# Decay tables woven into the first projection, and q of the first direction loaded in alternating pieces

## The chip, the cores and the metric

The program runs on one core of a Trainium2 chip. The metric is the time of one execution on the device in microseconds (us). Work is done by TensorE (PE; its weight loads are listed as PEld), VectorE (DVE), ScalarE (ACT) and GpSimd (POOL). Transfers between the chip's main memory and the on-chip memory of 128 rows (partitions) are issued by SyncE (SP) and by POOL, each in its own order, and run on 16 DMA engines which all queues share.

## The reference

The input x has 8 samples of 56 x 56 positions with 192 channels. Four layers follow each other, each of the form x = x + layer(group norm of x). Layers 0 and 1 are the ones concerned here. Each computes, with D = 576 channels:

```
p, q, v = silu(x @ p_w.T + p_b), silu(x @ q_w.T + q_b), silu(x @ v_w.T + v_b)
a1 = mlp1(lags) * decay ;  a2 = mlp2(lags) * decay      # (111 lags, D): one value per lag and channel
o1 = toeplitz(q * v, a1) along the width ;  o2 = toeplitz(q * v, a2) along the height
out = (p * (o1 + o2)) @ o_w.T + o_b
```

toeplitz(y, a) is, per channel, y multiplied by the 56 x 56 matrix that has a(i - j) at row i and column j. The decay of a lag n is a power n of a number per channel. Layer 2 is a depthwise 7 x 7 convolution with a two-layer product, layer 3 a window attention. Everything is float32.

## The kernel before, in words

The two Toeplitz layers are cut into generators which a hand-written weaver interleaves. `tno_qv` (called Q) projects two pairs of samples to q and v and stores q*v in main memory (`qv`); its products are at L260, or at L281 for the first 512 positions, where the two pairs are done one after the other (`apart`). `tno_toeplitz` (TZ) multiplies by the Toeplitz matrices, and `tno_out` (O) makes p, the gate and the output product. Per layer there are two halves of the batch (`j0` 0 and 2). The stages are: Q(0,0) alone; TZ(0,0) woven with Q(0,2); TZ(0,2) woven with O(0,0) and Q(1,0); TZ(1,0) woven with O(0,2) and Q(1,2); TZ(1,2) woven with O(1,0); and the last O woven with the convolution of layer 2.

**The start.** `input_stats` loads x of each of four pairs in seven tiles (L119, seven buffers) and DVE takes their statistics (L215). Q(0,0) starts when pair 0 has its norm. `decay_tables` (L134 on) makes the tables of one layer: powers of the decay on DVE, then for each of two directions three small products through the mlp (L179) and five products for the channels (L185), each followed by DVE's writes of the tile `a` (L192, two buffers) and by two to four stores of `a` into the table in main memory (L202, 36 stores per layer, 120 KB each). Each table step is built without a pause in the program: first all of layer 0 after 24 steps of Q, then 14 steps of Q with the statistics of pairs 2 and 3, then all of layer 1. A zero tile is made ahead of layer 1's tables and POOL copies it (L715) into the rows of `qv` behind the 56 x 56 positions, since loads of the second direction fetch 64 rows, and (L719) into the end of each table. In this part a scheduler orders each engine's instructions by their dependencies and by their place in the program; in the Toeplitz stages the compute engines follow the order of the program.

**Toeplitz.** A stage has 18 steps: nine blocks of 64 channels, two directions each. A step needs a q tile of 128 rows (q*v of two times 64 channels and samples: rows 0 to 55 and 64 to 119 are used; two buffers) and a matrix tile `tm` (two, used in turn). For the first direction rows of q are positions along the width: two transfers (L376), each of 56 rows with 56 runs of 512 bytes. For the second direction one transfer (L379) of 128 rows of 28,672 bytes. `tm` comes in four transfers of 32 rows of 7,680 bytes, for every fourth row each (L389). All are issued by SP, and a step's loads are issued when the last product of the step two before has been issued. SP waits for what an instruction needs before it goes on to the next, and the built order shows that each of its transfers also waits for the one eight before it. Products are at L402, ACT takes them out of PSUM (L409), DVE transposes them (L420, L422), and POOL adds the second direction (L424) and stores the sum.

The lines of q's load before the change:

```
for half in range(2):
    of = qv[2 * blk + half, :T].rearrange("(h w) e -> w h e", w=W)
    nc.sync.dma_start(q[64 * half : 64 * half + W], of)
```

Of the kernel before, what the change touches and what calls it, by code (L numbers as in the profile page):

```python
# [38 lines left out]
def view(ap, offset, dims):  # L39

    return bass.AP(ap.tensor, ap.offset + offset, [ap.ap[0], *dims])


class Net:
# [91 lines left out]
    def decay_tables(self, L, p, tables):  # L136
# [5 lines left out]
        for c in range(5):  # L142
            m = min(128, D1 - 128 * c)
            sl = p.tile([128, 1], F32, name="sl")
            nc.sync.dma_start(sl[:m], inp[f"{L}_slope"][128 * c : 128 * c + m, :])
            nc.vector.tensor_scalar(sl[:m], sl[:m], 0.0, 1.0, ALU.max, ALU.min)
            nc.vector.tensor_scalar(sl[:m], sl[:m], 1.0 - 0.95, 0.95, ALU.mult, ALU.add)
            pw = p.tile([128, 64], F32, name="pw", bufs=5)
            nc.gpsimd.memset(pw[:m, 0:1], 1.0)
            n = 1  # L150
            while n < 64:
                nc.vector.tensor_scalar(
                    pw[:m, n : 2 * n], pw[:m, 0:n], sl[:m], None, ALU.mult
                )
                n *= 2
                if n < 64:
                    sq = p.tile([128, 1], F32, name="sl")
                    nc.vector.tensor_mul(sq[:m], sl[:m], sl[:m])
                    sl = sq
            pows.append(pw)  # L160
        for d in range(2):
            t = f"{L}_t{d + 1}"
            w0 = p.tile([32, 2], F32, name="w0")
# [13 lines left out]
            for i in range(3):  # L177
                hp = self.bank2()[:32, 0, :111]
                nc.tensor.matmul(hp, ws[:, i, :], h, start=True, stop=True)  # L179
                h = p.tile([32, 111], F32, name="h")  # L180
                nc.vector.tensor_scalar(h, hp, bs[:, i : i + 1], 0.0, ALU.add, ALU.max)
            for c in range(5):
                m = min(128, D1 - 128 * c)
                ap = self.bank2()[:, 0, :111]
# [15 lines left out]
                for n in range(m // 32):  # L200
                    to = tables[d][self.TG * (4 * c + n) : self.TG * (4 * c + n + 1)]
                    nc.sync.dma_start(  # L202
                        to.rearrange("g (c w) -> c g w", w=self.TW),
                        view(a[32 * n : 32 * n + 32], 0, [[4, self.TG], [1, self.TW]]),
                    )

    def input_stats(self, xs, gn, j, p):

# [153 lines left out]
    def tno_toeplitz(self, j0, mats, qv, o):  # L362
# [6 lines left out]
        def load(n):  # L369
            blk, d = divmod(n, 2)  # L370
            q = p.tile([128, H, 128], F32, name="q", bufs=2)
            if d == 0:

                for half in range(2):
                    of = qv[2 * blk + half, :T].rearrange("(h w) e -> w h e", w=W)
                    nc.sync.dma_start(q[64 * half : 64 * half + W], of)  # L376
            else:
                of = qv[2 * blk : 2 * blk + 2].rearrange("n (h w) e -> (n h) (w e)", w=W)
                nc.sync.dma_start(q.rearrange("p i e -> p (i e)"), of)  # L379
            return q  # L380

        def matrices(n):

            blk, d = divmod(n, 2)
            row = 32 * self.TW
            at = mats[d].offset + 2 * blk * self.TG * row
            for k in range(4):
                of = bass.AP(mats[d].tensor, at + k, [[row, 2 * self.TG], [1, row]])
                nc.sync.dma_start(self.tms[n % 2][k:128:4], of)  # L389

        def along(n, q, ot, g):

# [44 lines left out]
        loaded = []  # L437
        for n in range(2):
            loaded.append(load(n))
            matrices(n)  # L440
        yield 8.0

        work = []
# [10 lines left out]
        for n in range(NS):  # L454
# [4 lines left out]
            for g in range(8):  # L459
# [5 lines left out]
                if g % 2:  # L465
                    if g == 7 and n + 2 < NS:
                        loaded.append(load(n + 2))
                        matrices(n + 2)
                    yield 3.2
                    behind()  # L470
        while work:
# [194 lines left out]
    def tno_layers(self, x0, x1, x2, gn, last):  # L666
# [18 lines left out]
        with ExitStack() as ctx, ExitStack() as wqp:  # L685
# [7 lines left out]
            with tc.tile_pool(name="tab", bufs=2) as tab:  # L693
# [10 lines left out]
                    pass  # L704
                for n in range(10):
                    next(first)
                self.decay_tables("L0", tab, tables[0])
                for st in stats[2:]:
                    for more in st:
                        next(first)  # L710
                none = tab.tile([112, 512], F32, name="none", bufs=1)
                nc.gpsimd.memset(none, 0.0)
                for qv in qvs.values():
                    to = qv[:, T:].rearrange("n (p k) e -> p n (k e)", p=112)
                    nc.gpsimd.dma_start(to, view(none, 0, [[0, D1 // 32], [1, 512]]))  # L715
                self.decay_tables("L1", tab, tables[1])
                for t in tables:
                    for d in range(2):
                        nc.gpsimd.dma_start(t[d][D1 // 32 * self.TG :, :512], none[:1])  # L719
                lanes = [[(first, QT - 104.0)], [(Q(0, 2), QT)], [(O(0, 0), OT), (Q(1, 0), QT)]]  # L720
                lanes += [[(O(0, 2), OT), (Q(1, 2), QT)], [(O(1, 0), OT)], [(O(1, 2, False), OT)]]
                self.weave(lanes[0], None, lanes[1][0][0])
            in_order = tc.manual_schedule(engines=ENGINES)
            with tc.tile_pool(name="tz", bufs=1) as self.tz, in_order:
                self.tms = []
# [915 lines left out]
```

## Time and profile before

| what | us |
|---|---|
| median of 3 runs (5851.6 to 5859.38) | 5857.68 |
| the profiled execution | 5859.99 |
| its span, first to last instruction | 5858.2 |
| PE busy in the span | 5356.5 (91%) |
| first product of Q(0,0) | 52.68 |
| first Toeplitz product (L402) | 507.7 |

The profile is of one execution. A line of the windows view gives the stretch, its length, and for PE, PEld, DVE, ACT and POOL the busy time with the number of instructions in brackets, then the mean granted clock of PE (1.00 is full), the mean busy share of the 16 DMA engines (packets overlap, so it can exceed 1) and GB/s. A line of the timeline gives start, length, engine, line of the code and operation; in square brackets the idle time before it and what ended it. SPq lines are the issue of transfers by SP, and their length is how long SP was held, not how long the data took. The trace also holds one record for each DMA packet, with its start, duration, size and queue.

### The profile page before, as it was taken

To read this page: it belongs to the slowest core of one execution; us is meant where nothing else is said; L and a number is where in the kernel's file an instruction comes from. 1 tells how busy PE (TensorE), PEld (TensorE's weight loads), DVE (VectorE), ACT (ScalarE), POOL (GpSimd) and SP (SyncE) were. 2 spreads that over 40 slices of the span, in tenths; PEclk is the share of its full clock that TensorE was granted. 3 is DMA by queue.
4 is the path that set the end of the run, shared out by engine and by line. 5 is a ranking of instruction groups with operands and counts; after the bars stand their busy time and mean duration, and the time that the engine had idled before them with its cause. 6 is when DMAs were issued, how large, how long until landed. Compare 5 with 4: busy or idle time off the path is not lost.

```text
span 5858.2 us, 144266 instructions
## 1 busy us (share of the span) xinstructions
PE 5356.5 (91%) x64672; PEld 3886.7 (66%) x64672; DVE 2365.6 (40%) x3770; ACT 2269.0 (39%) x2990; POOL 2206.4 (38%) x1527
## 2 busy tenths in 40 slices
PE   5799888899999999999888799989999999889887
PEld 2577666677777777777666578856665445667666
DVE  5444554233454233553343322331222322556655
ACT  2244454444454444554444322242323333333332
POOL 1244566466556564565666300000001001333332
PEclk8799999999999999999999899999999999999998
DMA  8547998898787887987999465644444222344442
GB/s 268 110 144 219 267 287 245 220 264 275 214 237 217 239 258 224 254 249 196 312 296 293 168 210 205 230 125 161 150 160 121 64 64 62 75 97 86 89 92 56
DMA packets 1029770, 1098.79 MB, mean 188 GB/s; under 512 B 232768, under 2 KB 966976, under 8 KB 1013728
## 3 DMA queue, kind: packets, MB, share of 16 engines
q1 hardware_dynamic: 993568, 888.57, 55.5%
q0 software_dynamic: 35584, 200.99, 8.9%
q8 instruction: 509, 8.34, 0.6%
q14 instruction: 109, 0.89, 0.0%
HBM read 725.48 MB, written 363.94 MB: 186 GB/s over the span
## 4 chain that ended last, share of the span: by engine, by line
PE 57%; POOL 6%; SPq 6%; DMA 5%; DVE 5%; issue 3%; ACT 2%; POOLq 0%; DVEq 0%; ACTq 0%
PE bank L260 9%; PE bank L950 6%; PE bank L811 5%; PE bank L527 4%; PE bank L1030 4%; PE bank L572 4%; PE bank L402 4%; SPq L389 3%; PE bank L1044 3%; POOL s L424 2%; PE bank L1224 2%; PE bank L536 2%; PE bank L575 2%; SPq L376 2%; PE bank L1171 2%
## 5 line engine op out<-in xcount | busy, mean ns | idle before, releaser
L260 PE MATMUL bank<-wq,t 128*128 128x256 f32 (+4 forms) x7680 | 1286.6, 375 | 66.8 <-DVE t L269 36.3
L260 PEld LDWEIGHTS bank<-wq,t 128*128 128x128 f32 (+2 forms) x7680 | 1006.5, 191 | 348.1 <-issue 110.5
L269 DVE TENSOR_TENSOR t<-bank,wq 128x1024 f32<-128x1024 f32 (+3 forms) x480 | 517.8, 1111 | 776.6 <-PE bank L260 575.1
L301 POOL TENSOR_TENSOR t<-t 128x1024 f32<-128x1024 f32 (+2 forms) x288 | 518.7, 1815 | 692.4 <-ACT t L298 371.5
L409 ACT COPY ot<-bank 128x896 f32<-128x896 f32 x576 | 493.2, 914 | 626.8 <-PE bank L402 351.3
L424 POOL TENSOR_TENSOR s<-s,ot 128x1568 f32<-128x1568 f32 x144 | 618.3, 4298 | 70.0 <-DVE ot L422 69.3
L402 PE MATMUL bank<-q,tm 56*32 56x224 f32 x18432 | 525.6, 365 | 81.6 <-DMA tm<-L_tab 26.8
L298 ACT ACTIVATE t<-t 128x2048 f32<-128x2048 f32 (+2 forms) x288 | 422.0, 1488 | 405.7 <-DVE t L269 396.1
L402 PEld LDWEIGHTS bank<-q,tm 56*32 56x32 f32 x18432 | 354.4, 109 | 221.6 <-issue 115.8
L553 POOL TENSOR_TENSOR t<-t,t 128x896 f32<-128x896 f32 x168 | 347.3, 2085 | 358.4 <-DMA t<-L_sum 163.9
L527 PE MATMUL bank<-t,wo 128*128 128x224 f32 x1792 | 398.0, 378 | 46.6 <-ACT t L506 22.1
L585 DVE SCALAR_TENSOR_TENSOR t<-bank,wo,t 128x448 f32<-128x448 f32 x112 | 76.4, 682 | 886.3 <-ACT t L581 474.7
L950 PE MATMUL bank<-z,w 128*128 128x448 f32 (+1 forms) x1344 | 413.7, 555 | 1.9 <-ACT h L959 1.7
L527 PEld LDWEIGHTS bank<-t,wo 128*128 128x128 f32 x1792 | 352.4, 203 | 83.8 <-issue 31.7
L546 ACT ACTIVATE t<-bank,wo 128x448 f32<-128x448 f32 x448 | 248.1, 635 | 407.2 <-PE bank L536 379.2
L572 PE MATMUL bank<-t,wo 128*128 128x224 f32 x1792 | 378.1, 365 | 0.0
L127 POOL DMA_DIRECT2D x<-x x64 | 36.6, 573 | 859.7 <-DVE x L981 829.6
L572 PEld LDWEIGHTS bank<-t,wo 128*128 128x128 f32 x1792 | 337.2, 194 | 33.8 <-issue 32.2
L811 PEld LDWEIGHTS bank<-xt,cm 113*112 113x112 f32 x3072 | 315.0, 180 | 43.7 <-issue 38.3
L420 DVE STREAM_TRANSPOSE s<-ot 128x1792 f32<-128x1792 f32 x144 | 292.5, 2033 | 124.3 <-DMA L_sum<-s 102.1
L811 PE MATMUL bank<-xt,cm 113*112 113x108 f32 (+2 forms) x3072 | 326.2, 266 | 6.4 <-issue 3.3
L950 PEld LDWEIGHTS bank<-z,w 128*128 128x128 f32 (+1 forms) x1344 | 182.2, 189 | 205.7 <-issue 197.4
(148 smaller groups left out, 6991.3 us busy)
## 6 DMA issues: line engine op xcount, KB each, us to landing
q<-qv SPq DMA_DIRECT2D x36, 3584.0 KB
q<-qv SPq DMA_DIRECT2D x72, 1568.0 KB
L_sum<-s POOLq DMA_DIRECT2D x288, 392.0 KB, 7.4
t<-L_sum SPq DMA_DIRECT2D x112, 1008.0 KB
qv<-t SPq DMA_DIRECT2D x192, 512.0 KB
cm<-in_L_cm SPq DMA_DIRECT2D x96, 896.0 KB
tm<-L_tab SPq DMA_DIRECT2D x288, 240.0 KB
x<-t POOLq DMA_DIRECT2D x112, 336.0 KB, 7.1
```

The source lines that it names most:

```text
L260: nc.tensor.matmul(pp[:m, b, 256 * j : 256 * j + k], x[rows, j, 2 if part else b, s : s + m], w[rows, part, c0 + c : c0 + c + k],  start=p ...
L269: nc.vector.tensor_add(z[:m, c : c + k, :], view(pp[:m], 0, [[1, k], [256, 4]]), view(bias[:m], c0 + c, [[1, k], [0, 4]]),)
L298: nc.scalar.activation(z[:m, :n, :], z[:m, :n, :], AF.Silu)
L301: nc.gpsimd.tensor_mul(prod[:m, :k], half[:, :, 0], half[:, :, 1])
L402: nc.tensor.matmul(pt[32 * j : 32 * j + 32, r, hf * 224 : (hf + 1) * 224], tm[rows, at : at + 32], q[rows, :, 4 * c : 4 * c + 4], start=Tr ...
L409: nc.scalar.copy(view(ot, 4 * (g % 4), [[16, 2], [32, 112], [1, 4]]), view(pt, 0, [[512, 2], [4, 112], [1, 4]]),)
L424: nc.gpsimd.tensor_add(to, to, view(of, 0, [[1, 28], [32, 56]]))
L527: mm(gs[c // 2][:, b, c % 2 * 256 : c % 2 * 256 + N], pw[:, 0, 128 * c : 128 * c + 128], xn[:, b], start=c % 2 == 0, stop=False,)
L553: gate.tensor_mul(to, to, pg)
L572: mm(P[:, b, :N], ow[:, c, 0:128], g[:, 4 * b + c], start=False, stop=c == 3 and b == 1)
L811: nc.tensor.matmul(pc[:, 128 * e + 4 * m0 : 128 * e + 4 * m1], cm[:113, e, k, :], xt[:, m0 - 1 + k : m1 - 1 + k, c + e, :], start=n == 0 a ...
L950: nc.tensor.matmul(phs[c][:, s, :TT], w0[rows, part, at : at + 128], z[rows, Z[2 if part else s], :], start=part == flip, stop=part != flip,)
```

## The change

Two parts. First, the generator `decay_tables` pauses after the powers, after each small product and after each table step, and both layers' tables become one stream. Fourteen of its steps are taken one by one with the steps of Q that go with the statistics of pairs 2 and 3; the others are woven into the rest of Q(0,0), spread over its first three quarters at a nominal total of 28.0 (there are 20 left of 1.0 each). The zeros for the tables come from a small tile of one row at the start; the zeros for `qv` come from one of the x buffers after the statistics.

Second, q of the first direction is loaded by eight transfers of 64 rows and 14 runs of 512 bytes, in turn to the lower and the upper rows, and the rows of `tm` for k = 0 come ahead of them in four transfers of eight rows; k = 1 to 3 follow behind. Rows 56 to 63 of a half receive what follows in `qv`; no product reads them. The second direction keeps its transfers.

```diff
@@ decay_tables
             pows.append(pw)
+            yield 1.0
...
                 nc.vector.tensor_scalar(h, hp, bs[:, i : i + 1], 0.0, ALU.add, ALU.max)
+                yield 1.0
...
+                yield 1.0
@@ tno_toeplitz
-            if d == 0:
-
-                for half in range(2):
-                    of = qv[2 * blk + half, :T].rearrange("(h w) e -> w h e", w=W)
-                    nc.sync.dma_start(q[64 * half : 64 * half + W], of)
+            tm, row = self.tms[n % 2], 32 * self.TW
+            at = mats[d].offset + 2 * blk * self.TG * row
+            of = lambda k: bass.AP(mats[d].tensor, at + k, [[row, 2 * self.TG], [1, row]])
+            if d:
+                qs = qv[2 * blk : 2 * blk + 2].rearrange("n (h w) e -> (n h) (w e)", w=W)
+                nc.sync.dma_start(q.rearrange("p i e -> p (i e)"), qs)
             else:
-                of = qv[2 * blk : 2 * blk + 2].rearrange("n (h w) e -> (n h) (w e)", w=W)
-                nc.sync.dma_start(q.rearrange("p i e -> p (i e)"), of)
+                for i in range(4):
+                    nc.sync.dma_start(tm[32 * i : 32 * i + 32 : 4], of(0)[8 * i : 8 * i + 8])
+                for i in range(0, H, 14):
+                    for half in range(2):
+                        qs = bass.AP(
+                            qv.tensor,
+                            qv.offset + ((2 * blk + half) * 64 + i) * W * 128,
+                            [[128, 64], [W * 128, 14], [1, 128]],
+                        )
+                        nc.sync.dma_start(q[64 * half : 64 * half + 64, i : i + 14], qs)
+            for k in range(1 - d, 4):
+                nc.sync.dma_start(tm[k:128:4], of(k))
             return q
-
-        def matrices(n):
-
-            blk, d = divmod(n, 2)
-            row = 32 * self.TW
-            at = mats[d].offset + 2 * blk * self.TG * row
-            for k in range(4):
-                of = bass.AP(mats[d].tensor, at + k, [[row, 2 * self.TG], [1, row]])
-                nc.sync.dma_start(self.tms[n % 2][k:128:4], of)
...
             loaded.append(load(n))
-            matrices(n)
...
                         loaded.append(load(n + 2))
-                        matrices(n + 2)
@@ tno_layers
-                self.decay_tables("L0", tab, tables[0])
+                none = tab.tile([1, 512], F32, name="none", bufs=1)
+                nc.gpsimd.memset(none, 0.0)
+                for t in tables:
+                    for d in range(2):
+                        nc.gpsimd.dma_start(t[d][D1 // 32 * self.TG :, :512], none)
+                decay = (dt for i in range(2) for dt in self.decay_tables(LS[i], tab, tables[i]))
                 for st in stats[2:]:
                     for more in st:
                         next(first)
-                none = tab.tile([112, 512], F32, name="none", bufs=1)
-                nc.gpsimd.memset(none, 0.0)
+                        next(decay)
+                rows = tab.tile([128, 3, TT], F32, name="x", bufs=7)[:112].rearrange("p k t -> p (k t)")
+                nc.gpsimd.memset(rows[:, :512], 0.0)
                 for qv in qvs.values():
                     to = qv[:, T:].rearrange("n (p k) e -> p n (k e)", p=112)
-                    nc.gpsimd.dma_start(to, view(none, 0, [[0, D1 // 32], [1, 512]]))
-                self.decay_tables("L1", tab, tables[1])
-                for t in tables:
-                    for d in range(2):
-                        nc.gpsimd.dma_start(t[d][D1 // 32 * self.TG :, :512], none[:1])
+                    nc.gpsimd.dma_start(to, view(rows, 0, [[0, D1 // 32], [1, 512]]))
...
-                self.weave(lanes[0], None, lanes[1][0][0])
+                self.weave(lanes[0], decay, lanes[1][0][0], 28.0, 0.0, 0.75)
```

## The prediction

> **What bounds the kernel.** I read the kernel in stretches (the windows view: PE busy and count, the same for PEld, DVE, ACT and POOL, then granted clock, DMA share, GB/s), because the busy shares of the page average over unlike stages.
>
> ```profile
> 50.00:100.00 50.00, 45.78 (x148) 19.92 (x148) 39.50 (x105) 14.30 (x24) 1.43 (x1) 0.93 0.64 217
> 100.00:150.00 50.00, 27.98 (x99) 12.72 (x98) 34.89 (x79) 21.34 (x23) 20.49 (x15) 0.74 0.89 219
> 150.00:200.00 50.00, 38.79 (x219) 30.83 (x220) 16.25 (x26) 10.27 (x8) 11.08 (x17) 0.88 0.50 113
> 200.00:250.00 50.00, 41.15 (x228) 31.92 (x227) 29.92 (x88) 21.30 (x24) 16.19 (x9) 0.84 0.44 127
> 250.00:300.00 50.00, 34.95 (x172) 25.63 (x173) 14.45 (x41) 8.16 (x6) 6.06 (x11) 0.73 0.51 84
> 300.00:500.00 200.00, 200.00 (x1246) 157.41 (x1242) 84.38 (x80) 87.44 (x89) 85.29 (x48) 1.00 0.51 145
> 507.00:1080.00 573.00, 480.31 (x6603) 362.56 (x6600) 268.76 (x194) 263.11 (x304) 330.53 (x187) 0.91 0.93 262
> 1080.00:1900.00 820.00, 790.67 (x8851) 606.87 (x8849) 333.78 (x352) 382.39 (x523) 479.11 (x293) 0.98 0.83 241
> 2740.00:3225.00 485.00, 430.76 (x6501) 327.21 (x6486) 187.55 (x195) 219.78 (x337) 304.75 (x191) 0.93 0.98 292
> ```
>
> PE sets the pace from 300 on, except in the first and last Toeplitz stages (507 to 1080, 2740 to 3225), where it is 16% and 11% idle and DMA is full. The two middle stages are PE's (96%). The head (to 300) is idle on PE in pieces, at a low clock. The timeline shows why:
>
> ```profile
> 1.99 2.43 POOL L715 DMA_DIRECT2D qv<-none  x2
> 41.49 1.68 DVE L215 BATCH_NORM_STATS2 st<-x 128x6 f32<-128x448 f32 x3 [4.77 <-DMA x<-in_x]
> 52.68 2.93 PE L281 MATMUL bank<-wq,t 128*128 128x512 f32 x3 [2.74 <-ACT t L243]
> 127.59 0.57 PE L179 MATMUL bank<-h,ws 32*32 32x111 f32 x2 [8.01 <-DVE h L181]
> 142.32 0.73 PE L185 MATMUL bank<-h,wo 32*128 32x111 f32 x2 [5.58 <-DVE a L192]
> 132.37 54.36 SPq L202 DMA_DIRECT2D L_tab<-a  x36
> ```
>
> Two zero fills of 4032 KB leave at 2 us and share the DMA with the first x, so the seventh x tile is measured at 41.49 and PE starts at 52.68. Later PE waits on the two blocks of decay tables (here the first), whose 36 stores hold SP for 54 us. In the last Toeplitz stage (SP, then PE):
>
> ```profile
> 2816.32 12.12 SPq L376 DMA_DIRECT2D q<-qv  x2
> 2828.49 11.91 SPq L389 DMA_DIRECT2D tm<-L_tab  x4
> 2840.57 0.47 SPq L499 DMA_DIRECT2D t<-L_sum  x1
> 2847.60 3.33 PE L402 MATMUL bank<-q,tm 56*32 56x224 f32 x64 [5.76 <-DMA tm<-L_tab]
> ```
>
> The load of a first-direction q holds SP for 24 us; from its issue to PE's use 31.3 us pass, more than PE has work for. This repeats every 55 us.
>
> The trace's DMA packet records say why it is slow. One such load is 2 x 56 x 56 = 6272 packets of 512 bytes. From 2824 to 2832 they start at 300 per us, each lasting 58 ns; all 6272 take 20.9 us. The qv stores' packets of the same size last 27 ns (31,643 of 34,816 from 300 to 480). Only about 2832 to 2834, where the lower rows end and the upper begin, does the rate rise, to 378 per us.
>
> [...] 14 four-byte packets close the lower half, 2831.5 to 2833.5. [...]
>
> **The change, part by part.** *Zero fills moved.* Ahead of PE's start remain seven x tiles (672 KB each), wq (1728 KB) and two t tiles (768 KB each): 7968 KB = 8.16 MB, at the 360 GB/s of the first 50 us 22.7 us. The x tiles alone (4.82 MB) take 13.4, after about 4 us to the first: last statistics near 17 instead of 41.49. The 11.2 us from there to PE stay: start at 28 instead of 52.7, **-25**. The fills now stand on POOL behind seven multiplies, their memset waiting for an x buffer, with later multiplies and their qv stores queued behind it. 8.26 MB is 23 us of DMA between some 80 and 130 us, beside traffic of 0.6 to 0.9: +5 (bounds 0 and 15; x of pairs 2 and 3 isn't urgent).
>
> *Decay tables woven in.* All of it is moved, none removed: 72 table stores and 36 small loads on SP, the DVE chain, POOL memsets and 32 small products on PE. From 150 to 300 PE has 619 records; 82 belong to the tables and to the norms, leaving 537 of L260. At 1246 per 200 us these need 86 us, the small ones 18: 104 of 150. Of 119.6 to 150 about 8 are work, 22 idle. So dense work saves 46 + 22 = 68. Against it: DVE's write of `a` waits for the four stores of the step two before (two buffers), and behind it on DVE stand the bias adds that free PSUM for PE. Four stores take 4 x 1.5 = 6 us (54.36 / 36) and a qv store about 1.2, while a unit of PE lasts 4.3 (80 records per three units): 3 us late on the third to fifth of five steps, in four directions, 12 x 3 = 36; PSUM's four buffers hide about a third: +24 (bounds 0 and 60). **-44.** Head in all 25 - 5 + 44 = **-64**, bounds -20 and -90.
>
> *q in eight transfers.* It adds six q transfers and three tm transfers per first-direction load; at 0.45 to 0.6 us each SP needs some 5 us more. These are hidden while earlier transfers run (SP is stuck for 24 us now). 64 rows read eight rows too many: 7168 packets, but on 16 engines instead of 14, so 448 per engine either way. What can shorten it is that halves alternate every 56 packets per engine[...]. [...] A piece alone takes 56 x 25.5 = 1.4 us (a 27 ns packet with the usual overlap); [...] Bounds: 12.1 (no conflict) and 23.9 (7168 at 300 per us). I take 15, as other packets disturb the offset: **-5.9 us a load**. Of 36 loads the 17 in the two DMA-full stages that aren't preloaded count: -100. The floors allow it: PE is busy 430.76 of 485 and 480.31 of 573, at mean clocks of 0.93 and 0.91. In the middle stages PE hides the load: -10. [...] 0.6 us x 17: +10. Without the cover of backlog the added issues would cost 5 us x 17 = 85.
>
> Sum: 5859.99 (the profiled execution; span 5858.2) - 64 - 100 = 5696; the median 5857.68 stands 2.3 below that execution: **5695**.
>
> **Rivals.** *In step.* Engines cross between halves together[...]; at 2832 the gain lasted only 2 us. The load stays near 21: 5858 - 64 + 10 = 5804. Against it: the offset of 1.2 us, and the start spread of 1.5 us seen in the records.
> *Tables stall PE.* `a` waits for stores at 1.5 us each; the head gives 20, q still 100: 5740. For it: L192 waits for stores already (28.6 us in all); against it: the second layer's steps are paced over half of the remaining stage.
> *[...] (slower).* The half's 300 packets per us is a ceiling and no mixing comes: 7168 / 300 = 23.9, +3.0 on each of 36 loads = 108, +10, -64: about 5910. It decides from 64 / 36 = 1.8 us a load upward; PE's slack in the middle stages speaks against the full 36.
> *Full gain.* No conflicts, 13.3 us a load: 17 x 7.6 = 129, middle stages 30, head 90: 5610.
>
> **How the numbers follow.** The forecast (own range 5640 to 5760) gets 0.52, in step 0.22, tables stall 0.07, slower 0.09, full gain 0.10. The range runs from 5620 to 5825: it leaves out the slower case and the far end of the full gain. 0.2% (12 us) is about what a measurement of this kernel can tell from no change. Faster: all but the slower case and 0.03 of in-step runs near zero: 0.88; same 0.03; slower 0.09.
>
> **What would show it.** Head: PE's first product near 28 us, Q's stage dense from 95, first L402 near 440 instead of 507; waits of DVE on L_tab stores show the table charge. q: 512-byte packets of the load back at 27 to 35 ns, over 400 per us; SP held under 18 us; the first and last stages shorter by 50 each, their clock over 0.95. Unchanged 53 ns packets with the same stage lengths mean in step; longer ones, the slower rival. I am wrong in kind [...] if DMA stays the bound at the same GB/s.

## The result, and the profile after

| | before | after |
|---|---|---|
| median of 11 runs each | 5857.68 us | 5842.75 us |
| profiled execution | 5859.99 | 5841.57 |
| first Toeplitz product | 507.7 | 458.7 |
| the four Toeplitz stages, first to last product | 501.3, 718.2, 718.3, 488.9 | 500.5, 728.0, 728.0, 492.0 |
| last Toeplitz product to the end | 2635.3 | 2641.8 |

The ratio is 0.9976, with a 95% interval from 0.9966 to 0.9986: 15 us faster. The forecast was 5695, range 5620 to 5825; the time lies outside. The head gained 49 us and kept it up to the first Toeplitz product; the four Toeplitz stages, which were to gain 100, together take 22 more. (The stretch of the last row, where nothing was changed, lies between 2623 and 2654 over the profiled executions of this study. So 10 us of a difference between two such executions say nothing, and in the extreme case 30; totals below are compared by their medians.)

The windows view of the kernel after, same columns as before; the stage windows are moved by the 49 us (first stage) and by the 28 us (last stage) by which these stages now start earlier:

```profile
50.00:100.00 50.00, 45.88 (x164) 21.44 (x160) 45.06 (x122) 21.61 (x26) 15.29 (x10) 0.90 0.58 185
100.00:150.00 50.00, 29.27 (x154) 22.75 (x154) 18.18 (x30) 13.76 (x14) 14.79 (x10) 0.79 0.81 263
150.00:200.00 50.00, 48.63 (x277) 38.94 (x276) 20.51 (x36) 18.94 (x19) 18.38 (x14) 0.91 0.53 132
200.00:250.00 50.00, 47.02 (x269) 36.64 (x268) 22.18 (x43) 21.33 (x23) 14.24 (x14) 0.93 0.58 137
250.00:300.00 50.00, 47.34 (x277) 36.25 (x278) 30.46 (x73) 21.95 (x24) 21.96 (x17) 0.97 0.50 136
300.00:500.00 200.00, 197.29 (x1635) 152.34 (x1634) 90.33 (x105) 87.82 (x92) 73.22 (x49) 0.99 0.73 185
458.00:1031.00 573.00, 470.38 (x6564) 359.66 (x6564) 265.28 (x189) 260.29 (x299) 327.34 (x184) 0.91 0.97 274
1031.00:1851.00 820.00, 790.32 (x8837) 607.16 (x8836) 334.92 (x355) 376.53 (x512) 474.18 (x291) 0.98 0.83 240
2712.00:3197.00 485.00, 422.08 (x6390) 324.23 (x6394) 186.96 (x194) 214.92 (x331) 301.65 (x189) 0.92 1.02 291
```

From 150 to 300 PE is dense now (143 of 150 instead of 115), as forecast. From 100 to 150 it is not. In the first and last Toeplitz stages PE is no busier: 470 instead of 480, 422 instead of 431, with DMA fuller (0.97 and 1.02).

The timeline of the kernel after, head (start, length, engine, line; in brackets the idle time before and what ended it):

```profile
27.99 22.56 PE L284 MATMUL bank<-wq,t 128*128 128x512 f32 x64 [2.74 <-ACT t L246]
109.00 1.15 POOL L724 DMA_DIRECT2D qv<-x  x1
122.49 29.85 SPq L307 DMA_DIRECT2D qv<-t  x9
139.80 3.03 POOL L304 TENSOR_TENSOR t<-z 128x1024 f32<-128x1024 f32 x2 [29.64 <-DMA qv<-t]
146.44 3.23 PE L263 MATMUL bank<-wq,t 128*128 128x128 f32 x16 [13.81 <-DVE t L272]
```

The start is where it was forecast, at 27.99. The second fill leaves at 109; POOL then waits 29.64 us for a store of q*v to free its buffer, DVE waits for POOL, and PE for DVE: 13.81 us idle. The stores themselves leave only from 122.49, because SP stands before that in fourteen transfers, most of them small loads for the tables and of the next weights, ten of them at about 2 us each. The timeline of the last Toeplitz stage:

```profile
2841.08 3.89 SPq L383 DMA_DIRECT2D tm<-L_tab  x4
2845.02 18.59 SPq L391 DMA_DIRECT2D q<-qv  x8
2863.66 4.20 SPq L393 DMA_DIRECT2D tm<-L_tab  x3
2874.59 3.36 PE L407 MATMUL bank<-q,tm 56*32 56x224 f32 x64 [7.36 <-DMA tm<-L_tab]
```

SP is held 26.7 us by one load (24.0 before), and from its issue to PE's use 33.5 us pass (31.3 before). In the view of waits, PE's waits for the two tiles of a step, 36.0 us before, are 42.7 after, all of it for the matrix tile. Before, then after (us in all, times, longest):

```profile
PE bank L402 <- DMA tm<-L_tab: 26.8, 6, 10.1
PE bank L402 <- DMA q<-qv: 9.2, 2, 5.0
```

```profile
PE bank L407 <- DMA tm<-L_tab: 42.7, 12, 7.5
```

For the packets of 512 bytes I use one measure for every kernel: the median over all stretches of 1 us in the first and last Toeplitz stages in which packets of no other size (but closing ones of four bytes) start. Where these stretches begin moves it by a few packets. Before: 307 per us, 56.4 ns each. After: 376 per us, 50.8 ns. How many engines carry a transfer I take from the four-byte packets that close it, one for each engine: the trace of before has 37,057 packets of four bytes, that of after 41,233, and the 4176 more are just 36 x (8 x 16 - 2 x 14 + 4 x 8 - 16): 16 for a transfer of 64 or 32 rows, 14 for one of 56 and eight for one of eight. Which engines these are, no record says. So a load of 7168 packets takes 19.1 us, where 6272 took 20.4; the forecast had 15.

### The profile page after: what moved, and what is told of

It is laid out like the page before. It is cut to its first block, busy times and chain, and to the rows that moved or that the text cites. A ratio compares the mean times of both kernels' runs of the same rounds, so it can differ in the third digit from the quotient of the medians.

```text
span 5839.7 us, 144665 instructions
## 1 busy us (share of the span) xinstructions
PE 5367.1 (92%) x64672; PEld 3902.7 (67%) x64672; DVE 2367.8 (41%) x3770; ACT 2267.8 (39%) x2990; POOL 2204.9 (38%) x1528
## 4 chain that ended last, share of the span: by engine, by line
PE 53%; DMA 8%; SPq 7%; POOL 6%; DVE 6%; issue 3%; ACT 2%; POOLq 0%; ACTq 0%; DVEq 0%
PE bank L263 8%; PE bank L955 6%; SPq L391 5%; PE bank L816 5%; PE bank L1035 4%; PE bank L530 4%; PE bank L575 4%; PE bank L407 3%; PE bank L1049 3%; DMA t<-L_sum 3%; POOL s L429 2%; DMA qv<-t 2%; PE bank L1229 2%; PE bank L539 2%; PE bank L578 2%
## 5 line engine op out<-in xcount | busy, mean ns | idle before, releaser
L407 PE MATMUL bank<-q,tm 56*32 56x224 f32 x18432 | 527.7, 367 | 99.4 <-DMA tm<-L_tab 42.7
```

The costliest lines, as they stand in the source:

```text
L407: nc.tensor.matmul(pt[32 * j : 32 * j + 32, r, hf * 224 : (hf + 1) * 224], tm[rows, at : at + 32], q[rows, :, 4 * c : 4 * c + 4], start=Tr ...
```

## The experiments

Runs of one group share runs of the kernel before on the same chip, and those medians lie between 5849 and 5860; so I compare gains against before, from each group's own. The medians are of 4 to 12 runs. "First Toeplitz" is the first Toeplitz product and "stages" the sum of the four Toeplitz stages, first to last product, both in the profile; "rate" is the measure just described. e4 and e5 don't compute the reference, since their q tile has other rows of `qv` in it.

| run | median | ratio, 95% interval | against before | first Toeplitz | stages | rate, ns |
|---|---|---|---|---|---|---|
| before | 5857.68 | | | 507.7 | 2427 | 307, 56 |
| after | 5842.75 | 0.9976, 0.9966 to 0.9986 | -15 | 458.7 | 2448 | 376, 51 |
| e1 head alone | 5802.38 | 0.9920, 0.9905 to 0.9935 | -51 | 457.7 | 2427 | 308, 56 |
| e2 q load alone | 5889.90 | 1.0061, 1.0048 to 1.0075 | +36 | 505.6 | 2446 | 374, 52 |
| e3 fills in pieces | 5802.46 | 0.9915, 0.9902 to 0.9928 | -51 | 451.1 | 2419 | |
| e4 one transfer, 128 rows | 5690.50 | 0.9722, 0.9709 to 0.9735 | -163 | 454.8 | 2310 | 566, 34 |
| e5 every second row | 5669.48 | 0.9683, 0.9668 to 0.9699 | -184 | 459.6 | 2296 | 568, 34 |
| e6 without the lead | 5771.42 | 0.9861, 0.9842 to 0.9880 | -82 | 456.9 | 2399 | 380, 51 |
| e7 56 rows, 8 pieces | 5746.06 | 0.9822, 0.9797 to 0.9847 | -107 | 453.7 | 2359 | 353, 48 |
| e8 SP and POOL | 5919.58 | 1.0121, 1.0094 to 1.0148 | +67 | 452.0 | 2537 | |
| e9 56 rows, 16 pieces | 5722.31 | 0.9771, 0.9748 to 0.9794 | -137 | 452.5 | 2329 | 392, 41 |
| e10 eight rows behind q | 5825.39 | 0.9941, 0.9918 to 0.9963 | -34 | 459.4 | 2441 | 380, 51 |
| e11 64 rows, 2 transfers | 5838.33 | 0.9967, 0.9953 to 0.9981 | -21 | 458.4 | 2460 | 344, 58 |
| e12 SP and ACT | 5794.41 | 0.9893, 0.9863 to 0.9923 | -65 | 451.6 | 2401 | 516, 33 |
| e13 as e9, fills behind tables | 5704.08 | 0.9744, 0.9726 to 0.9763 | -145 | 440.2 | 2334 | |
| e14 lead by columns | 5790.93 | 0.9901, 0.9880 to 0.9921 | -59 | 451.9 | 2407 | 378, 51 |
| e15 SP and ACT, tm too | 5965.84 | 1.0199, 1.0180 to 1.0217 | +116 | 472.2 | 2522 | 516, 33 |
| e16 56 rows, 28 pieces | 5719.30 | 0.9776, 0.9761 to 0.9791 | -130 | 452.5 | 2343 | 405, 34 |
| e17 every fourth row | 5845.59 | 0.9989, 0.9980 to 0.9997 | -7 | 459.3 | 2455 | 307, 55 |
| e18 as e17, fills behind tables | 5817.56 | 0.9950, 0.9937 to 0.9964 | -35 | 442.3 | 2447 | 308, 55 |

**First group: which part of the change did what.**

e1, the change without its q load:

```diff
-                for i in range(4):
-                    nc.sync.dma_start(tm[32 * i : 32 * i + 32 : 4], of(0)[8 * i : 8 * i + 8])
-                for i in range(0, H, 14):
...
+                for half in range(2):
+                    qs = qv[2 * blk + half, :T].rearrange("(h w) e -> w h e", w=W)
+                    nc.sync.dma_start(q[64 * half : 64 * half + W], qs)
-            for k in range(1 - d, 4):
+            for k in range(4):
```

> Only the first part of the change (fills moved, tables woven); q of the first direction is loaded as before, by two transfers of 56 rows. Theory A, the head keeps what it gained and the new q load gives half of it back: the first Toeplitz product stays near 458.7, the four Toeplitz stages keep their length of before, 5859.99 - 49 = about 5810. Theory B, the new q load is neutral and the 49 us are lost again in the Toeplitz stages by themselves, since an earlier start meets another alignment of loads: about 5835 to 5845, as with both parts.

e2, the kernel before with the new `load` and nothing else of the change.

> Only the second part: q of the first direction in eight transfers of 64 rows behind four of eight rows of tm; the head as before. Theory A: the Toeplitz stages together are longer by 25 to 30, about 5885. Theory B: within 5 us of before.

The head alone gains 51 and its stages are as long as before (2427 us); the q load alone loses 36, most of it in the stages (+20 in the profile, which was its fastest run; the two middle ones +13 and +9). The two add up to the result: -51 + 36 = -15 (the intervals of both are some 8 us wide to either side, so the exact fit is luck). Theory A holds, B falls: the new load isn't neutral, it takes back 70% of what the head gives.

e3, the head alone with the fills cut up and put behind the tables in the program:

```diff
-                    to = qv[:, T:].rearrange("n (p k) e -> p n (k e)", p=112)
-                    nc.gpsimd.dma_start(to, view(rows, 0, [[0, D1 // 32], [1, 512]]))
+                def zeros():
+                    for n in range(D1 // 32):
+                        for qv in qvs.values():
+                            to = qv[n, T:].rearrange("(p k) e -> p (k e)", p=112)
+                            nc.gpsimd.dma_start(to, rows[:, :512])
+                        yield 1.0
```

> As the run with the head alone, and the zero fills of qv in 36 pieces of 224 KB, two at a time, behind the last table step in the rest of the first projection (18 more steps). Theory C, the two fills of 4032 KB from 98 to 130 us cause the 13.8 us wait of PE at 132.6 and the low clock after it (the stores of POOL's products stand behind 15 small transfers of SP that share the DMA with the fills): the stretch from 100 to 150 is 45 busy instead of 29, the first Toeplitz product comes 20 to 25 earlier than with the head alone, near 436, total near 5787. Theory D, the small loads of the tables alone hold the stores: no change at the first Toeplitz product, total as with the head alone.

This run didn't test what it was made for. On POOL the pieces still left from 97 us on, as nothing they need was late and POOL was free: the scheduler put them ahead of their place in the program. The first Toeplitz product came 7 us earlier, the total was that of e1. e13 repeats it properly. But e3 has one use: in it the stores of q*v stand between the small loads on SP and not behind them, while the fills still run. PE's long wait, in e1 and then in e3:

```profile
144.95 3.23 PE L263 MATMUL bank<-wq,t 128*128 128x128 f32 x16 [12.14 <-DVE t L272]
```

```profile
128.71 13.67 PE L263 MATMUL bank<-wq,t 128*128 128x256 f32 x72 [10.60 <-DVE t L272]
```

e4, q of the first direction in one transfer; its upper rows take the rows of `qv` that follow the lower ones, and not those of the other half:

```diff
+                qs = bass.AP(
+                    qv.tensor,
+                    qv.offset + 2 * blk * 64 * W * 128,
+                    [[128, 128], [W * 128, H], [1, 128]],
+                )
+                nc.sync.dma_start(q, qs)
```

> The head as after; q of the first direction in one transfer of 128 rows with 56 runs of 512 bytes each. The upper rows take other values of q*v than they should (the rows that follow in qv), so that the pattern has three steps; number and size of packets are those of 64 rows in each half. Theory E, a half of the rows takes at most some 300 packets per us and both at once twice that: 512-byte packets at 27 ns, 550 to 600 per us, a load of 12 to 13 us, the first and last Toeplitz stages 40 shorter each: about 5720. Theory F, scattered 512-byte reads themselves go no faster than 360 per us: load near 20 us and about 5810.

Theory E holds: 566 packets per us at 34 ns, 163 us faster than before, 112 faster than the head alone. The first and last stages take 458 and 440 instead of 502 and 492 (e1). The windows view of its last stage, and a load in its timeline:

```profile
2620.00:3105.00 485.00, 437.71 (x6622) 335.22 (x6620) 202.16 (x214) 227.16 (x354) 346.09 (x212) 0.97 0.93 316
```

```profile
2681.86 1.98 SPq L387 DMA_DIRECT2D q<-qv  x1
2683.90 20.02 SPq L389 DMA_DIRECT2D tm<-L_tab  x4
2704.09 2.17 SPq L498 DMA_DIRECT2D t<-L_sum  x2
```

In these two stages the last packet of tm lands 22 and 24 us after the load's issue (medians; 28 and 30 in e1). In the last one DMA moves 316 GB/s where it moved 291, and the clock is at 0.97. So the size of the prize was right (112 against e1; the rival of a full gain had 129 and 30 for q); the way to it in the change was not. This form can't be used as it is, since in the true data the upper rows don't follow the lower ones at the step of this pattern.

**Second group: what hinders the packets.**

e5, as e4 with two transfers of 64 rows, to the even and to the odd rows of the tile:

```diff
...
-                nc.sync.dma_start(q, qs)
+                for odd in range(2):
...
+                    nc.sync.dma_start(q[odd:128:2], qs)
```

> The head as after; q of the first direction in two transfers of 64 rows, the first to the even and the second to the odd rows of the whole tile, so that each transfer writes both halves. As in the run with one transfer of 128 rows, rows take other values of q*v than they should; number and size of packets stay. Theory G, each engine serves neighbouring rows of a transfer [...], as the prediction had it: eight engines write below, eight above all the time, 560 packets per us, about 5690 as with one transfer. Theory H, the rows of a transfer go around the engines in turn, so that all engines write the lower half first and then the upper: 300 to 360 per us, about 5800.

568 per us at 34 ns. Theory G holds: both halves are written at once within one transfer. It isn't a matter of one transfer of 128 rows, but of both halves being under way all the time. Nor is it the source, although e4 and e5 read fewer different rows of `qv`: the first transfer of a load in e5 reads the very rows that the first one in e11 below reads, with 565 to 568 packets per us in that transfer already (in the load after 2769), and e11, which writes these rows into one half, has 344.

e6, after without the lead:

```diff
-                for i in range(4):
-                    nc.sync.dma_start(tm[32 * i : 32 * i + 32 : 4], of(0)[8 * i : 8 * i + 8])
-            for k in range(1 - d, 4):
+            for k in range(4):
```

> As after, without the lead of four transfers of eight rows: eight q transfers of 64 rows and 14 runs in turn below and above, then tm in four transfers of 32 rows. Theory I, the lead sets the two groups of eight engines apart and part of the 360 packets per us is its work: 300 to 330 per us without it, load 22 to 24 us, total 5860 to 5890. Theory J, the lead does nothing for the rate, the extra over 300 comes where one piece ends and the next begins, and the lead costs SP and the engines 2 to 4 us a load: about 5800 to 5820.

Theory J: the rate is the same without the lead (380 and 376), and the program is 67 us faster (-82 against -15). The offset which the forecast built on (by my estimate the lead keeps eight engines busy for 4 x 0.291 = 1.2 us before their first q, and the other eight not) does nothing for the rate.

e7, e6 with 56 rows per transfer (`[128, 64]` becomes `[128, W]`):

> As the run without the lead, with 56 rows in each of the eight transfers instead of 64 (6272 packets instead of 7168, 14 engines). If the rate stays at 360 per us the load takes 17.4 us, 3.5 less than before, and with 17 loads about 60 are gained over the head alone: 5745. If the rate falls to 14/16 of that (315 per us), the load takes 19.9 and the gain is about 17: 5785. If eight transfers cost more than two by themselves: above 5802.

The rate is 353, so a load takes 17.8 us; gain 25 over e6, total as the first of the three cases had it. The eight rows that nobody reads, and the two more engines that come with them, cost 25 us here.

e8, the two transfers of before, the upper one issued by POOL (`nc.gpsimd`):

> The head as after; the two transfers of 56 rows of before, the upper issued by POOL and the lower by SP, so that both are under way at once and each engine takes packets from both. Theory E (a limit for each half of the rows): engines write below and above in turn or mixed, 450 to 550 packets per us, load 12 to 14 us, 5700 to 5740. [...] Third way: POOL's issue of 3136 runs, or its wait for the last product of the step, delays the additions behind it, above 5810.

The third way, for a reason not foreseen. POOL's transfer went out as packets of 4096 bytes, some 38 per us at 385 ns, as soon as POOL got there, and was nearly through when SP's half began: in the load that POOL issued at 2814.3, SP's 512-byte packets came up to 300 per us at 2830, when other loads ahead of them in SP's queue were done. While POOL's packets ran, SP's 896-byte packets came down to some 30 per us. The halves were not under way together, so the run doesn't tell what two queues could do; e12 does.

**Third group: pieces, the lead, rows, queues.**

e9, e7 with 16 transfers of 7 runs (`14` becomes `7`):

> As the run with 56 rows in eight transfers, with 16 transfers of 7 runs. Theory K, the rate over 300 per us comes only where all engines go from one half to the other: with twice as many changes it rises from 365 to about 430, load 14.6 us instead of 17.2, about 5715. Theory L, the engines stand at fixed, uneven distances spread over a whole piece, [...] whatever the piece: rate 360 to 380 as with eight, 5740 to 5755; eight more issues of 0.4 to 0.5 us on SP are hidden. If SP's issues count, above 5760.

392 per us at 41 ns, 30 us faster than e7. The rate rises with the number of changes between halves, as K had it, but by little more than half of what K gave. The waits of PE in e9 (all stages):

```profile
PE bank L405 <- DMA tm<-L_tab: 10.4, 3, 6.4
```

Of 42.7 us of PE's waits for tm in the kernel after, 10.4 are left.

e10, e6 with the eight-row transfers of k = 0 behind q instead of one of 32 rows:

> As the run without the lead (5771), with the tm rows of k = 0 in four transfers of eight rows again, but behind the q transfers. Theory M, the lead cost 72 us because it stands ahead of q: the q packets share their first 2 us with it (140 to 220 per us there) and all of q comes later: without that place the time is that of the run without the lead, 5765 to 5780. Theory N, transfers of eight rows on eight engines and three more issues cost by themselves wherever they stand: 5820 to 5845.

N: 47 us slower than e6 though nothing stands ahead of q any more. Theory M falls; the place is not what costs most (e10 is 19 faster than after).

e11, e1 with 64 rows per transfer:

> The head as after; q in two transfers as with the head alone, of 64 rows instead of 56, no pieces and no lead. The ceiling of one half (the slower rival of the prediction): 300 packets per us, 7168 / 300 = 23.9 us instead of 20.9, 3 us times 17 to 28 loads over 5802: 5850 to 5890. If 16 engines instead of 14 carry it: 343 per us, 5802.

344 per us, not 300: with 64 rows the half takes 16 engines' packets at the same 56 to 58 ns each as 14 engines' with 56 rows. So a half has no ceiling of 300; a load takes 20.8 us (20.4 in e1). The rate is that of the second case, the total is not: 30 us are lost (-21 against -51), stages 33 longer. The extra packets are 896 x 36 = 32,256 of 512 bytes in stages where DMA is full (0.97 and 1.02 in the kernel after).

e12, e8 with ACT in POOL's place (`nc.scalar`):

> The head as after; the two transfers of 56 rows, the upper issued by ACT and the lower by SP. ACT has by then copied the last product of the step, so its issue waits for nothing new. If both queues are under way together and each engine takes packets of both: 450 to 550 per us, load 12 to 14 us, 5700 to 5740 less what ACT is held by the issue (0.5 to 10 us a load; where that is 10 us, PE waits for PSUM and the total is above 5800). If one queue finishes before the other: as with the head alone, 5802, or more.

516 per us at 33 ns, on 14 engines: with two such queues the halves do mix (from 2770 to 2775 each queue starts some 258 packets per us), and packets are as short as in e4. Two queues into the same half were not run, so this run alone can't tell the halves from the second queue. ACT is held 0.3 us by each issue. The gain over e1 is 14 all the same, and the two intervals overlap: SP's half begins behind SP's other loads (in the load issued at 2757.7 its packets begin at 2767), and tm lies behind it.

**Fourth group.**

e13, e9 with the fills' source made from the last table:

```diff
-                nc.gpsimd.memset(rows[:, :512], 0.0)
...
+                    nc.gpsimd.dma_start(rows[:, :512], tables[1][1][end - 112 : end, :512])
+                    nc.gpsimd.tensor_scalar(rows[:, :512], rows[:, :512], 0.0, None, ALU.mult)
...
```

> As the run with 16 pieces (5722), and the zero fills of qv in 36 pieces whose source tile is made from a row block of the last table, so that none can leave before the tables are done (in the run with late fills they left from 97 us on). Theory C, the fills cause the wait of PE near 130: the stretch from 100 to 150 is 43 to 47 busy instead of 30, first Toeplitz product near 430 instead of 451, total about 5702. Theory D, the 15 small loads of the tables in one row on SP with the stores behind them cause it: 30 to 36 busy, first Toeplitz product above 443, total 5715 to 5722.

The windows view of e13:

```profile
100.00:150.00 50.00, 46.70 (x266) 36.97 (x267) 24.62 (x44) 23.57 (x25) 18.94 (x11) 0.90 0.49 150
```

46.70 busy instead of 29.27 in the kernel after, no wait of PE over 4.3 us in that stretch, and the last product of Q(0,0) ends 17 us earlier than in e9 (435.2, 452.6). PE then waits 5.0 us for `tm`, so the first Toeplitz product is 12 earlier (440.2, 452.5). Theory C holds at the head: without the fills the wait is gone. The same small loads are there, and SP is held 0.4 to 1.2 us by each instead of 2. Their order on SP has changed too, since the stores of q*v now stand between them:

```profile
106.66 0.38 SPq L307 DMA_DIRECT2D qv<-t  x1
107.15 0.52 SPq L240 DMA_DIRECT2D t<-in_x  x1
109.97 1.05 SPq L307 DMA_DIRECT2D qv<-t  x2
111.08 1.21 SPq L174 DMA_DIRECT2D bo<-in_L_t_bo  x1
```

But in e3, with stores between the loads as well and the fills still running, PE's wait was 10.60 us, against 12.14 in e1; so the order explains little of it. At the end, 8 of the 12 us show against e9 (-145 and -137), inside the two intervals. With 5704 (0.9744) this is the best kernel here that computes the reference, ahead of before by 145 us and of after by 131.

e14, after with the lead in four transfers of 32 rows by a quarter of their columns:

```diff
-                for i in range(4):
-                    nc.sync.dma_start(tm[32 * i : 32 * i + 32 : 4], of(0)[8 * i : 8 * i + 8])
+                for i in range(0, row, row // 4):
+                    nc.sync.dma_start(tm[0:128:4, i : i + row // 4], of(0)[:, i : i + row // 4])
```

> As after, with the lead in four transfers of 32 rows and a quarter of their columns (1920 bytes per row) instead of four of eight whole rows: as many transfers, as many bytes, at the same place, over 16 engines instead of eight. If the number and place of the transfers cost: as after, 5830 to 5850. If the eight engines that carry a double part cost: as the run without the lead, 5765 to 5785. Both in halves: near 5805.

-59: of the lead's 67 us, 44 go when the same bytes at the same place, in as many transfers, go over 32 rows at a time; 23 stay for the place and the three more transfers. That agrees with e10 (47 for the eight-row form behind q). The packets of this lead are of 1920 bytes instead of 7680, so their size is in the 44 too.

e15, e12 with tm of k = 1 and 3 on ACT too:

> As the run with upper q by ACT and lower q by SP (5794), and of the four tm transfers of a first-direction load the second and fourth by ACT too. In that run the packets of both halves went at 516 per us and 33 ns, but SP's half began behind its other loads, and tm behind it. If the late tm is what is left: the last tm lands 3 to 5 us earlier and the total is 5730 to 5760. If ACT, whose copies of PSUM stand behind its issues, is what costs: 5795 or more.

The packets are as quick as in e12 and the program is 181 us slower than e12. ACT's timeline tells why:

```profile
2873.80 0.32 ACTq L384 DMA_DIRECT2D q<-qv  x1
...
2874.22 14.81 ACTq L386 DMA_DIRECT2D tm<-L_tab  x2
2889.14 1.71 ACT L407 COPY ot<-bank 128x896 f32<-128x896 f32 x2 [14.34 <-issue]
```

ACT, issuing two more transfers behind a large one of its own, stands there for 14.8 us, and the PSUM copies with it. One transfer per load holds ACT for 0.3 us, three hold it for 15.

e16, e9 with 28 transfers of 4 runs:

> As the run with 16 pieces (5722), with 28 transfers of 4 runs. If the rate keeps rising with the number of changes between halves (353 at 8, 392 at 16): 420 to 440, 5700 to 5715. If the distances limit it: 390 to 400 and 5720 to 5730. If SP's issues become the limit (28 times 0.45 to 0.6 = 13 to 17 us a load, beside tm's): above 5735.

405 per us; 130 faster than before, as e9 within their intervals. The rate has nearly stopped rising with the number of pieces. But the packets last 34 ns here, as in e4 and e12, and not 41, and the engines are no longer full: by the packet records of the same stretches in the last stage, each of the 14 has 1.03 packets under way (median), where before, after, e4, e7, e9, e12 and e13 have 1.20 to 1.24 for each engine that a transfer uses. So it is no longer slow packets that hold the rate. SP issues the 28 transfers of a load in 18 to 23 us, half of all within 0.53 us of the one before, with 224 packets each, and 224 / 0.53 = 420 per us; whether SP's pace sets the rate or the rate sets SP's pace (in the built order each transfer waits for the one eight before it) isn't shown.

**Last group: is it neighbouring rows?** In the trace of the kernel after I looked at the four-byte packets that close each engine's part of a transfer (16 per piece, a piece every 2.4 us). In the load with its packets from 2858 to 2866.5 they come in two groups of eight, 1.5 and 0.9 us apart, which is what the lead was meant to do; there the rate is 367 and a packet takes 50.4 ns. In the load from 3021 to 3030 all 16 come within 1.2 us; there the rate is 380 and a packet takes 51.2 ns. So the distance of the two groups makes no difference, and I took it that engines within a group hinder each other.

e17, e1 with every fourth row of a half in a transfer:

```diff
-                    nc.sync.dma_start(q[64 * half : 64 * half + W], qs)
+                    for k in range(4):
+                        nc.sync.dma_start(q[64 * half + k : 64 * half + W : 4], qs[k:W:4])
```

> The head as after; q of the first direction in eight transfers of 14 rows, every fourth row of a half each (k, k + 4, ...), all 56 runs, the lower half first and then the upper, no row too many. Theory P, the rows of a transfer go around the engines in turn [...], while an engine alone makes 35 (566 / 16): with every fourth row [...] 14 engines make 14 x 35 = 495 per us at 34 ns, though all write the same half. Load 12.7 us instead of 20.4, total near 5680. Theory Q, the half of the rows is the limit [...]: 300 to 345 per us as before, total 5790 to 5810.

Theory P falls: 307 per us at 55 ns, exactly as with neighbouring rows. The run says less than it was made for, though. P had the rows go around the engines in turn, and e5 had already spoken for neighbouring rows on one engine. If that is so, each engine writes the same four neighbouring rows of a half here, one in each transfer, as it writes in one transfer in e1 (an estimate from e5's 568 per us; the records name neither rows nor engines). Whether another choice of rows within one half is faster isn't tested. The total is 45 us above e1 at the same packet rate (stages 28 longer, 12 to 15 of it in each middle stage): eight transfers in place of two aren't free, though the load takes no longer in its packets.

e18, e17 with the fills as in e13:

> As the run with every fourth row, and the fills of qv behind the tables as in the run with 16 pieces and late fills. Theory P and C together: 17 less than that run, near 5663. Theory Q: near 5785.

Theory C again: first Toeplitz product at 442.3 instead of 459.3, and 28 us gained over e17.

## Why the prediction was wrong, step by step

**The start (-25): right.** First product at 27.99, forecast 28.

**The tables (-44): near in sum, by luck, and only seen without the fills.** In e13 the last product of Q(0,0) ends 507.7 - 435.2 = 72 us earlier than before, and the first Toeplitz product comes 67 earlier; -25 and -44 make -69. Its two terms were both off and cancel: by e13 dense work saved 72 - 25 = 47 and not 68, and the +24 for waits on table stores didn't come at all. DVE's wait for them, 28.6 us in all before, is absent from the waits of the kernel after, and there PE waits 7.4 us in all from 150 to 456 us.

**The zero fills (+5, bounds 0 and 15): wrong in size.** They delay the end of Q(0,0) by 17 us (e13 against e9) to 20 (e18 against e17), beyond the bound, and the first Toeplitz product by 12 and 17. The step named the right queue, POOL, and the right traffic, and took the DMA share as the whole price. What it left out is SP: it was held by each small load of the tables for about 2 us instead of 0.4 while the fills ran, fourteen transfers stand ahead of the stores of q*v, and POOL has no buffer until those are stored. So the head gained 49 and not 64.

**q in eight transfers (-100): wrong, +36 instead (e2); this is the step that failed.** The load was to fall from 20.9 us to 15; by the rate it takes 19.1, and three costs beside it were put at 10 or at nothing. Its parts, taken one after the other from e1 over e11 and e6 to after:
- *64 rows for 56, "448 packets per engine either way".* Right for the packets (344 against 307 per us), but the step gave it no price; e11 puts it at +30.
- *Halves in turn.* This gains, 60 us (e6 against e11), less than forecast: 380 per us. The load was to take 15 us; this was my estimate, that with an offset of 1.2 us two groups of eight engines write opposite halves most of the time and don't slow each other, and no trace showed it. The closing packets show an offset of this kind in one load and none in another, with the same packet time; e6 without the lead has the same rate. In the trace of before all 14 closing packets of the lower half come between 2831.3 and 2833.2, after 9 us of packets. So no engine of a half was through early, and all were slowed alike; why, no run tells.
- *The lead, "0.6 us x 17 = +10".* It cost 67 (e6 against after): 1.9 us on each of 36 loads. Its 7680-byte packets were assumed to last 291 ns; in the load after 2846 the first seven last 291 to 306, later ones beside q's packets up to 879, and the 512-byte packets come down to some 130 to 200 per us there. The eight-row form is 44 of the 67 (e14). The middle stages, counted out, pay too: after against e6 +14 and +11.
- *Issues hidden at nothing.* Eight transfers for two at an equal packet rate: 45 us in e17. How much of that is in the pieces of e6, e7 and e9 isn't separated.

**Middle stages (-10).** They are 10 us longer each (718 to 728).

**The sum.** 5696 less 2.3 is 5693.7 and not 5695; this changes nothing.

**The rivals.** *In step* (5804) was nearest: its load of 21 us (19 measured) and packets of 53 ns (51) came true, but it put only +10 on the side of the cost. Its name is not what was shown, since loads in step and out of step were equally slow. *The slower rival's* ceiling of 300 per us for a half is refuted by e11's 344. *Full gain* had the right price for both halves at once: e4 and e5 reach 5690 and 5669 with the head's fills still in the way, against 5610 with a head of 90 that didn't come.

**Signs.** Of those named: start at 28 yes; dense from 95 no, from 150; first Toeplitz product near 440 no, 459; 27 to 35 ns and over 400 per us no, 51 and 376; SP held under 18 no, 26.7; stages shorter by 50 each no, 0.8 shorter and 3.1 longer; clock over 0.95 no, 0.91 and 0.92. The sign "unchanged packets with the same stage lengths" is what came.

## What to carry to other kernels

Before splitting or reordering a load, find out what the packets do in the best pattern, by a kernel that loads as many packets in that pattern and leaves out that they be the right rows: e4 gave the size of the prize in one run, and e1 with e2 showed that one part of a change was spending what the other earned. Turn taking between halves paid here in many small pieces with no extra rows and no small transfers on few engines: so made, the same idea is 122 us better than in the kernel after (e9, -137, against -15). And a transfer that "has time" must be given a real dependency if it is to wait; in an automatically ordered part its place in the program doesn't hold it (e3: the fills left from 97 us on).

## What the runs showed of the hardware that was not expected

- Packets of 512 bytes into one half of the rows last 55 to 58 ns, whether 14 or 16 engines write (307 and 344 per us) and whether a transfer has neighbouring rows or every fourth (e1, e11, e17). Into both halves within one transfer they last 34 ns: at 566 per us in e4, with one transfer over all rows, and at 568 in e5, whose transfers take every second row of all 128. For 16 engines each that is 566 / 344 = 1.65 times the rate into one half.
- With separate transfers for the two halves, halves in turn from SP alone give 380 per us against 344 in eight pieces of 64 rows (e6 and e11, +10%), and 405 against 307 in 28 pieces of 56 rows (e16 and e1, +32%). With one half from SP and one from ACT it is 516 per us at 33 ns (e12).
- POOL's transfer of runs of 512 bytes went out in packets of 4096 bytes (e8), SP's and ACT's in packets of 512.
- Why alternation ends near 400 per us, where half of the engines could be in each half, is open. With eight and 16 pieces the packets are slow (51 and 41 ns); with 28 they are not (34 ns), and the engines are less full (1.03 packets under way instead of 1.20 in e9).
